# A shared root for two norms: ten GpSimd instructions become four steps on ScalarE and GpSimd, in a new written-out order

## The chip, the cores and the metric

The kernel runs on one core of a Trainium2 chip. The metric is the time of one execution in microseconds (us), taken on the device. Engines are named as in the profile: PE is TensorE's matmul, PEld its weight load, DVE is VectorE, ACT is ScalarE, POOL is GpSimd, SP is SyncE.

## What is computed

Two layers on an image batch x of shape 4 x 256 x 256 x 64 (batch, height, width, channels), float32. Cut to what matters:

```python
def ln(x, g, b):                      # norm over the 64 channels
    mu = mean(x, -1); var = mean((x - mu)**2, -1)
    return (x - mu) * rsqrt(var + 1e-3) * g + b

# layer 0
h  = ln(x, g1, b1) @ w_te + b_te                    # 64 -> 128 channels
F  = fft2(h)                                        # over height and width
fc = gelu(concat(F.real, F.imag) @ w_fc + b_fc)     # 256 -> 256
sp = ifft2(fc[..., :128] + 1j * fc[..., 128:]).real
x1 = x + sp @ w_tp + b_tp
h2 = ln(x1, g2, b2) @ w_fe + b_fe
d  = gelu(depthwise_conv3x3(h2) + b_dw)
x2 = x1 + d @ w_fp + b_fp
# layer 1: moving average over height, plus a filter of the rest with
# complex weights in the frequency domain; here one 256 x 256 matrix per channel
out = layer1(x2)
```

There are two norms: the first feeds the forward transform, the second feeds the 3 x 3 convolution. Each needs one over the square root of a variance for every pixel. The change is about how that root is computed.

## The kernel before

**Tiling and stages.** The work is cut into three kinds of pieces, and all three run in a pipeline. *Forward chunks* f(n), 32 per image, 128 in all: load four columns of x (`fl`), norm, half-sums, and the transform along the height (`y0`, `y1`), evicted by `yt0`, `yt1` and stored to memory. *Pairs* k, 65 per image, 260 in all: transform along the width (`x`), copy to SBUF (`xs`), the mixing matmuls (`m0`, `m1`), evictions (`gc0`, `gc1`), sums and differences on VectorE (`b0`, `b1`), Gelu on ScalarE (`g0`, `g1`), a sum on GpSimd (`p0`, `p1`), the projection `z` with its copy `zs`, a transpose `w` with its copy `zt`, and the way back along the width (`u`, `us`, `uc`, and `uf`, which stores u). *Convolution chunks* c(n), 32 per image: load u (`ul`, or `UL` for an image's first chunk) and x (`xl`, `XL`), back along the height (`s`), residual (`r0`, `r1`), second norm, transposes (`t0`, `t1`) with copies (`tt0`, `tt1`), row sums on GpSimd (`T0`, `T1`), products (`gm`, `gh`, `em`, `eh`), their evictions (`gc_0`, `gc_1`, `ec0`, `ec1`) and sums (`cf0`, `cf1`, `sp0`, `sp1`), Gelu (`a0`, `a1`), projection (`o0`, `o1`, copies `fs0`, `fs1`), transposes back (`ft0`, `ft1`) and the final sum and store (`st0`, `st1`). Layer 1 comes after all this, from about 3900 us.

**The order of the work** is written out by hand. A list of operations with offsets rules one period n; an entry such as `m0:2` means "do m0 up to index 2 beyond this period's base" (for pairs the base is 2(n - 35), for the way back n - 35, else n). There are lists for four stretches: SPECTRUM (forward chunks and pairs), FULL (all three kinds together: the stretch "beside the first transform", periods 71 to 131), MIXED (pairs and convolution, 132 to 169), CONV (convolution alone). `do(op, k)` runs an operation once for every index up to k, and first whatever FOLLOWS says must come ahead of it (`fx fp` means that fx needs fp of the same index). If no PSUM bank is free, the operation that frees the oldest one is pulled forward (`make_room`). PE, DVE, ACT and POOL run strictly in the order in which the program emits their instructions. Period 103 has no convolution chunk, since an image's first chunk needs the whole way back of its image.

**The norms.** `statistics` makes the operations of both norms. For the first norm (side 0) they are `fq fr fR fm fM fp` and then `fx`, for the second (side 1) `cq cr cR cm cM cp` and then `cx`: square (ACT, line 275), sum (DVE, line 279), the mean's square put beside the squares (ACT, lines 284 and 285), variance (DVE, line 290), start of the root (DVE, line 309), root (POOL), and the scaling of the data by the root (POOL, line 352). In the stretch FULL a forward chunk and a convolution chunk share a *round* (`get`): whichever sum comes first opens the round, the other side joins it. Then `cM` makes an integer seed for 32 columns (16 of each side), and `cp` refines it with ten GpSimd instructions, lines 330 to 340, two steps of a Newton kind. `fM` and `fp` of side 0 do nothing there. Elsewhere side 0 takes the power -0.5 in one GpSimd instruction (line 325), and side 1 the ten instructions with 16 columns. `rooted`, called by the scaling, takes the power for one chunk if its root isn't there yet, and clears the open round.

Of the kernel before, what the change touches and what calls it, by code (L numbers as in the profile page):

```python
# [11 lines left out]
F32 = mybir.dt.float32  # L12
I32 = mybir.dt.int32
AF = mybir.ActivationFunctionType
ALU = mybir.AluOpType
# [4 lines left out]
P = 128  # L20
# [116 lines left out]
def conv_seq_kernel(ctx: ExitStack, tc: tile.TileContext, a: dict, tables: bass.AP, out: bass.AP):  # L137
    nc = tc.nc
    x = a["x"]
# [4 lines left out]
    shared = ctx.enter_context(tc.tile_pool(name="shared", bufs=1))  # L144
# [57 lines left out]
    def const(shape, name):  # L202
        return consts.tile(shape, F32, tag=name, name=name)
# [19 lines left out]
    make_identity(nc, ident)  # L223
    minus_half = const([P, 1], "minus_half")
    nc.vector.memset(minus_half, -0.5)

    wp = const([P, 2 * HID], "wp")
    b_fc = const([P, 2], "b_fc")
# [13 lines left out]
    edge_rows = const([P, 2], "edge_rows")  # L242

    ROWS = 16
    joint = {"on": False, "open": None}
# [4 lines left out]
    def statistics(index, src, name, side):  # L250

        state = {}
        own = slice(side * ROWS, (side + 1) * ROWS)
        both = slice(0, 2 * ROWS)

        def get(j):
            if j not in state:
                round_ = joint["open"] if joint["on"] else None
                if round_ is None or side in round_["sides"]:
                    round_ = {"sides": set(), "done": set(), "has": set()}  # L260
                    for tag, bufs in (("total", 3), ("var", 3), ("seed", 3)):
                        round_[tag] = shared.tile(
                            [P, 2 * ROWS], F32, tag=tag, name=f"{tag}_{name(j)}", bufs=bufs
                        )
                    joint["open"] = round_ if joint["on"] else None
                else:
                    joint["open"] = None
                round_["sides"].add(side)
                round_[side] = j, index
                state[j] = round_  # L270
            return state[j]

        def square(j):
# [18 lines left out]
        def cols_of(j, alone):  # L292

            s = get(j)
            if alone:
                return s, own
            if side == 0:
                return s, None if joint["on"] or len(s["sides"]) == 2 else own
            if joint["open"] is s:
                joint["open"] = None  # L300
            if 0 not in s["has"]:
                s["has"].add("apart")
            return s, own if "apart" in s["has"] else both

        def start_root(j):
            s, cols = cols_of(j, False)
            if cols is not None and side:
                var, seed = s["var"][:, cols], s["seed"][:, cols]
                nc.vector.tensor_scalar(
                    seed.bitcast(I32), var.bitcast(I32), -0.5, float(0x5F3759DF), ALU.mult, ALU.add  # L310
                )

        def root(j, alone=False):
            s, cols = cols_of(j, alone)
            if cols is None:
                return
            n = cols.stop - cols.start
# [4 lines left out]
            var, seed, rstd = s["var"][:, cols], s["seed"][:, cols], rstd[:, cols]  # L322
            state.pop(j)
            if alone or not side:
                nc.gpsimd.tensor_tensor(rstd, var, minus_half.to_broadcast([P, n]), ALU.pow)
                return
            t = shared.tile([P, 2, 2 * ROWS], F32, tag="newton", name=f"newton_{name(j)}", bufs=1)
            t0, t1 = t[:, 0, cols], t[:, 1, cols]
            tt, ts = nc.gpsimd.tensor_tensor, nc.gpsimd.tensor_scalar
            tt(t0, seed, seed, ALU.mult)  # L330
# [6 lines left out]
            ts(t1, t0, 0.375, -1.25, ALU.mult, ALU.add)  # L337
            tt(t1, t1, t0, ALU.mult)
            ts(t1, t1, 1.875, None, ALU.add)
            tt(rstd, t1, rstd, ALU.mult)  # L340

        def rooted(j):
# [5 lines left out]
        return (square, add, less_mean, variance, start_root, root), rooted  # L348

    def scale(src, dst, rstd):  # L350
        n = src.shape[1]
# [140 lines left out]
    def forward_h(pool):  # L492
# [104 lines left out]
        def part(f, i):  # L597
# [2 lines left out]
        both = (("fh", halves_h), ("y", transform), ("yt", evict))  # L600
        return {
            "fl": load,
            **dict(zip(("fq", "fr", "fR", "fm", "fM", "fp"), stats)),
            "fx": scaled,
            "fa": halves,
            "fb": quarters,
# [289 lines left out]
    def convolution(pool, pairs):  # L896
# [386 lines left out]
        def when(f, is_first):  # L1283
# [10 lines left out]
            "s": back_h,  # L1294
            "r0": residual_even,
            "r1": residual_odd,
            **dict(zip(("cq", "cr", "cR", "cm", "cM", "cp"), stats)),
# [194 lines left out]
    def is_late(j):  # L1492
# [2 lines left out]


    FOLLOWS = """
        fq fl | fr fl | fR fr fq | fm fq fR | fM fm | fp fM | fx fp | fa fx y0:-1 y1:-1 | fb fa
# [3 lines left out]
        cc cl | c0 UL | xl st0:-6 st1:-6 | XL st0:-6 st1:-6 | s ul UL c0 | r0 s xl XL | r1 r0 | cq r1 | cr r1 | cR cr cq | cm cq cR | cM cm | cp cM  # L1502
# [18 lines left out]
    for line in FOLLOWS.replace("\n", "|").split("|"):  # L1521
# [3 lines left out]


    FULL = numbered("""
        gc1:1 b1:1 w:-2 cm:-1 gh:-4 gc_0:-4 cf0:-4 a1:-5 m0:1 cr:-1 gc0:1 zs:-1 b0:1 t0:-2 tt0:-2 fl
        fp:-1 fq fr fh0:-2 u:-1 us:-1 ul t1:-2 s cl uc:-1 fm cc:-1 tt1:-2 x:2 xl XL r0 zt:-2 w:-1
        g0:1 zt:-1 gc_1:-4 o1:-5 x:3 xs:2 fs1:-5 cR:-1 g1:1 r1 cq m0:2 o0:-5 p1 fR fx:-1 sp0:-4  # L1530
        sp1:-4 xs:3 fh1:-2 y0:-2 yt0:-2 fs0:-5 fM z ft0:-5 cM:-1 ft1:-5 cf1:-4 gc0:2 zs b0:2 m1:2
        gc1:2 st0:-5 y1:-2 yt1:-2 T0:-2 T1:-2 p1:1 Ta:-2 a0:-4 em:-3 g0:2 b1:2 eh:-3 fa:-1 fb:-1
        ec0:-3 ec1:-3 m1:3 p0:1 z:1 st1:-5 cp:-1 gm:-3 g1:2 uf:-1 p0:2 cx:-1 UL:1
    """)

    MIXED = numbered("""
        t0:-2 a0:-5 xs:1 zt:-3 gm:-4 t1:-2 tt0:-2 a1:-5 p0:-2 p1:-2 z:-2 zs:-2 gh:-4 uf:-2 cM:-1
        p0:-1 gc_0:-4 cf0:-4 g1:-1 cp:-1 m1 gc1 b1 s cl tt1:-2 r0 gc_1:-4 m0 gc0 m0:1 p1:-1 z:-1
        gc0:1 r1 x:2 b0 xs:2 o1:-5 fs1:-5 u:-1 o0:-5 T0:-2 x:3 cq b0:1 us:-1 fs0:-5 g0 cr cR uc:-1
        w:-2 ul:1 xl XL ft0:-5 zs:-1 st0:-5 ft1:-5 st1:-5 em:-3 g0:1 T1:-2 Ta:-2 eh:-3 zt:-2 ec0:-3  # L1540
        ec1:-3 m1:1 sp0:-4 sp1:-4 cx:-1 w:-1 cf1:-4 gc1:1 g1 b1:1 cm cc:-1 UL:1
    """)

    CONV = numbered("""
# [195 lines left out]
```

## Time and profile before

| | |
|---|---|
| time, median of 3 runs | 4371.74 us (4369.35 to 4373.44) |
| the profiled execution | 4370.57 us |
| its span, first to last instruction | 4368.8 us |
| PE, DVE, ACT, POOL busy over the span | 96%, 79%, 66%, 76% |
| granted TensorE clock, mean | 0.985 |
| MB read, written | 364.81, 286.00 |

A row of the profile names a line of the program, the engine, the operation, the tiles written and read, their shape and type and the count; after the bar come the busy time in us and the mean of one in ns, and after a second bar the idle time of the engine just ahead of them and what ended it. A busy PE isn't PE at its peak, since matmuls are pipelined and their ends are modelled. The chain of work goes back from the last instruction to whatever released it; each piece has its start, its length and what it was.

### The profile page before, as it was taken

How to read it: one execution, taken by the hardware profiler on the slowest of the kernel's cores; microseconds unless marked ns; L12 is line 12 of the kernel's file. 1: busy time of each engine (PE TensorE's matmuls, PEld its weight loads, DVE VectorE, ACT ScalarE, POOL GpSimd, SP SyncE). 2: the span in 40 equal slices, each digit the busy share in tenths (PEclk: the TensorE clock that was granted, in tenths of full speed). 3: DMA queues.
4: the chain of work that ended last, by engine and by line, in shares of the span. 5: the costliest groups of instructions: out<-in, count | busy, mean ns of one | idle time of the engine just before them, and what ended most of it. 6: DMA issues, size and time to landing. Idle time of an engine off the chain costs nothing.

```text
span 4368.8 us, 67589 instructions
## 1 busy us (share of the span) xinstructions
PE 4183.0 (96%) x22443; PEld 2308.1 (53%) x22443; DVE 3453.4 (79%) x5227; ACT 2892.5 (66%) x5121; POOL 3315.0 (76%) x3509
## 2 busy tenths in 40 slices
PE   8989999889999999899999999999998799999999
PEld 4544444345555555455555566666665466664444
DVE  6968999689999988898888877888887699972222
ACT  3338998677777777677777777888886366641111
POOL 6869999699999999799999877888887588850000
PEclk9999999999999999999999999999999899999999
DMA  6664555434444444444444343444433534439886
GB/s 187 210 188 140 160 160 161 139 102 132 134 136 135 131 124 129 125 127 135 135 136 126 111 112 97 117 111 111 117 102 82 174 105 113 117 91 372 343 344 230
DMA packets 763907, 655.30 MB, mean 150 GB/s; under 512 B 46413, under 2 KB 657695, under 8 KB 755240
## 3 DMA queue, kind: packets, MB, share of 16 engines
q1 hardware_dynamic: 726696, 583.84, 45.5%
q10 hardware_dynamic: 36864, 67.13, 4.0%
q8 instruction: 181, 2.97, 0.3%
q14 instruction: 166, 1.36, 0.1%
HBM read 364.81 MB, written 286.00 MB: 149 GB/s over the span
## 4 chain that ended last, share of the span: by engine, by line
PE 78%; DVE 9%; POOL 4%; ACT 4%; DMA 3%; issue 2%; SPq 1%; DVEq 0%; POOLq 0%; ACTq 0%
PE ps_p L692 10%; PE ps_o L1446 10%; PE ps_h_c L1108 9%; PE ps_h_c L1122 5%; PE ps_x L667 5%; PE ps_f_c L1225 5%; PE ps_u L798 5%; PE ps_s_c L983 5%; PE ps_y L557 4%; PE ps_z L747 4%; PE ps_hh_c L1108 4%; PE ps_zt L765 3%; PE ps_t_c L1030 3%; PE ps_ft_c L1250 2%; PE ps_hh_c L1122 2%
## 5 line engine op out<-in xcount | busy, mean ns | idle before, releaser
L712 DVE TENSOR_TENSOR g<-ps_p,g 128x512 f32<-128x512 f32 x1040 | 707.6, 683 | 131.1 <-ACT g L706 110.1
L723 POOL TENSOR_TENSOR g<-g 128x512 f32<-128x512 f32 (+1 forms) x520 | 677.0, 1313 | 126.3 <-ACT g L717 115.9
L717 ACT ACTIVATE g<-g,b_fc 128x1024 f32<-128x1024 f32 (+1 forms) x520 | 600.3, 1156 | 3.2 <-DVE g L712 3.1
L692 PE MATMUL ps_p<-xs,wp 64*128 64x512 f32 (+1 forms) x2080 | 566.5, 616 | 13.1 <-ACT xs L682 7.2
L1108 PE MATMUL ps_h_c<-td,wc_main 128*128 128x256 f32 x2048 | 506.8, 390 | 0.7 <-ACT zs L755 0.3
L1108 PEld LDWEIGHTS ps_h_c<-td,wc_main 128*128 128x128 f32 x2048 | 369.7, 192 | 143.2 <-ACT h_c L1142 41.4
L706 ACT COPY g<-ps_p 128x512 f32<-128x512 f32 (+1 forms) x520 | 304.4, 585 | 211.1 <-PE ps_p L692 140.8
L1446 PE MATMUL ps_o<-xc,mt 128*128 128x512 f32 x1024 | 441.5, 594 | 1.2 <-DVE oc L1460 1.2
L1218 ACT ACTIVATE h_c<-h_c,b_conv 128x1024 f32<-128x1024 f32 x256 | 295.5, 1156 | 128.3 <-DVE h_c L1187 51.0
L1460 DVE TENSOR_SCALAR oc<-ps_o,b_fp 128x512 f32<-128x512 f32 x128 | 93.4, 749 | 347.1 <-DMA out_dram<-oc 175.4
L1070 POOL TENSOR_TENSOR td<-tt 128x512 f32<-128x512 f32 x256 | 324.6, 1290 | 10.0
L551 POOL TENSOR_TENSOR xb<-xt 128x512 f32<-128x512 f32 x224 | 286.2, 1285 | 56.4 <-DVE xt L544 37.2
L1446 PEld LDWEIGHTS ps_o<-xc,mt 128*128 128x128 f32 x1024 | 195.1, 191 | 247.0 <-issue 236.6
L1458 ACT ACTIVATE oc<-ps_o,b_fp 128x512 f32<-128x512 f32 x128 | 86.1, 686 | 358.6 <-PE ps_o L1446 190.8
L667 PEld LDWEIGHTS ps_x<-tab,yb 128*64 128x64 f32 x4064 | 229.1, 137 | 153.3 <-issue 43.5
L1122 PE MATMUL ps_h_c<-td,wc_half 64*128 64x256 f32 (+1 forms) x2048 | 293.2, 401 | 2.4 <-POOL td L1074 1.0
L1264 DVE TENSOR_TENSOR st<-x_c,ps_ft_c 128x256 f32<-128x256 f32 x512 | 259.8, 596 | 40.4 <-PE ps_ft_c L1250 40.4
L1225 PE MATMUL ps_f_c<-h_c,w_fp 128*64 128x512 f32 x1024 | 273.7, 621 | 15.8 <-ACT h_c L1218 14.6
L747 PE MATMUL ps_z<-g,w_tp 128*64 128x512 f32 x1024 | 275.8, 610 | 13.3 <-POOL g L723 9.0
L983 PE MATMUL ps_s_c<-uc_c,tab 64*128 64x512 f32 x1024 | 260.8, 622 | 21.5 <-DVE uc_c L932 13.3
L692 PEld LDWEIGHTS ps_p<-xs,wp 64*128 64x128 f32 x2080 | 185.1, 186 | 182.1 <-issue 67.8
L557 PE MATMUL ps_y<-xb,tab 128*64 128x512 f32 x1024 | 265.3, 610 | 12.6 <-POOL xb L551 10.3
(189 smaller groups left out, 9654.3 us busy)
## 6 DMA issues: line engine op xcount, KB each, us to landing
y_d<-yt SPq DMA_DIRECT2D x256, 256.0 KB, 2.6
yb<-y_d SPq DMA_DIRECT2D x256, 256.0 KB, 4.2
u_d<-ut SPq DMA_DIRECT2D x256, 256.0 KB, 3.9
x_c<-in_x_dram SPq DMA_DIRECT2D x512, 128.0 KB, 3.2
x_d<-st SPq DMA_DIRECT2D x128, 512.0 KB, 4.8
xc<-x_d SPq DMA_DIRECT2D x64, 1024.0 KB, 8.1
out_dram<-oc ACTq DMA_DIRECT2D x256, 256.0 KB, 5.7
xt<-in_x_dram SPq DMA_DIRECT2D x504, 128.0 KB, 2.5
```

Of the source, the lines that this page charges most:

```text
L557: nc.tensor.matmul(ps[i * C : (i + 1) * C], dh[:, m, i * C : (i + 1) * C], sums[j][:, i], start=True, stop=True,)
L667: nc.tensor.matmul(ps[r * C : (r + 1) * C, j * N + t * P : j * N + (t + 1) * P], blk[:, t, k, r * C : (r + 1) * C], tb[:, t, :], start=Tru ...
L692: nc.tensor.matmul(ps[:, :nf], wp[rows, cols], rhs[rows], start=True, stop=r == 1 or not pr["special"],)
L712: nc.vector.tensor_tensor(gt[:, i], re, gt[:, 1], op)
L717: nc.scalar.activation(g, g, AF.Gelu, bias=b_fc[:, half : half + 1])
L723: nc.gpsimd.tensor_tensor(g[:, 0], g[:, 0], g[:, 1], op)
L747: nc.tensor.matmul(ps[r * C : (r + 1) * C, :nf], w_tp, d[:, :nf], start=True, stop=True)
L983: nc.tensor.matmul(pss[i], tb[i * C : (i + 1) * C], uc[i * C : (i + 1) * C, ::-1, 1 - r, :] if down else uc[i * C : (i + 1) * C, :, r, :], ...
L1108: nc.tensor.matmul(product(j, k, par), wc_main[:, par, k, :], td[:, k, slots(j)].rearrange("p j q -> p (j q)"), start=k in (0, 1, 3), stop ...
L1122: nc.tensor.matmul(product(j, k, par)[:, dst.start * Q : dst.stop * Q], wc_half[lo : lo + C, k, :], td[lo : lo + C, k, src].rearrange("p j ...
L1225: nc.tensor.matmul(ps[par * C : (par + 1) * C], w_fp, gs[j][:, :, par, i0 : i0 + 2, :].rearrange("p r j q -> p r (j q)"), start=True, stop ...
L1446: nc.tensor.matmul(ps[:, :nf], mts[i // CM][:, i % CM, t, to * P : (to + 1) * P], xc[:, t, :, :, i, :], start=t == 0, stop=t == 1,)
```

## The change

In the stretch FULL the shared root is no longer ten GpSimd instructions in one operation, but four operations of the list, `cA`, `cB`, `cC` and `cp` (with `fA`, `fB`, `fC`, `fp` of side 0, which do nothing there). Each has one or two activations on ScalarE and one multiplication on GpSimd, on 32 columns. The second step's polynomial is brought into the form of a square plus a constant. The list FULL is new throughout. MIXED is the same cyclic order, begun at another place, with the offsets that this brings; the last index of `gm` and `em` in it sets from which chunk on the convolution takes its late form (166, before 167). Outside FULL the roots are computed as before. The scratch tile `newton` has two buffers instead of one.

```diff
+    affine = const([P, 3], "affine")
+    nc.vector.memset(affine[:, 0:1], 1.5)
+    nc.vector.memset(affine[:, 1:2], -(0.375**0.5) * 5.0 / 3.0)
+    nc.vector.memset(affine[:, 2:3], 5.0 / 6.0)
...
         def start_root(j):
-            s, cols = cols_of(j, False)
-            if cols is not None and side:
+            s = get(j)
+            s["whole", side] = joint["whole"] or side == 0 and not joint["on"]
+            s["spread", side] = joint["on"]
+            cols = s["cols", side] = None if s["whole", side] else cols_of(s)
+            if cols is not None:
...
+        def square_seed(j):
...
+            a, t = (s["t", side][:, i, cols] for i in range(2))
+            nc.scalar.activation(a, s["seed"][:, cols], AF.Square)
+            nc.gpsimd.tensor_tensor(t, a, s["var"][:, cols], ALU.mult)
+
+        def first_step(j):
...
+            s["rstd", side] = roots(s, j)
+            a, t = (s["t", side][:, i, cols] for i in range(2))
+            nc.scalar.activation(a, t, AF.Identity, bias=affine[:, 0:1], scale=-0.5)
+            nc.gpsimd.tensor_tensor(
+                s["rstd", side][:, cols], a, s["seed"][:, cols], ALU.mult
+            )
+
+        def square_step(j):
...
+            a, t = (s["t", side][:, i, cols] for i in range(2))
+            nc.scalar.activation(a, s["rstd", side][:, cols], AF.Square)
+            nc.gpsimd.tensor_tensor(t, a, s["var"][:, cols], ALU.mult)
+
+        def root(j, alone=False):
+            s = get(j)
+            if alone or s["whole", side]:
...
+            if not s["spread", side]:
+                in_place(roots(s, j)[:, cols], s["var"][:, cols], s["seed"][:, cols], j)
+                return
+            a, t = (s["t", side][:, i, cols] for i in range(2))
+            rstd = s["rstd", side][:, cols]
+            nc.scalar.activation(a, t, AF.Square, bias=affine[:, 1:2], scale=0.375**0.5)
+            nc.scalar.activation(a, a, AF.Identity, bias=affine[:, 2:3])
+            nc.gpsimd.tensor_tensor(rstd, a, rstd, ALU.mult)
...
     FULL = numbered("""
-        gc1:1 b1:1 w:-2 cm:-1 gh:-4 gc_0:-4 cf0:-4 a1:-5 m0:1 cr:-1 gc0:1 zs:-1 b0:1 t0:-2 tt0:-2 fl
-        fp:-1 fq fr fh0:-2 u:-1 us:-1 ul t1:-2 s cl uc:-1 fm cc:-1 tt1:-2 x:2 xl XL r0 zt:-2 w:-1
-        g0:1 zt:-1 gc_1:-4 o1:-5 x:3 xs:2 fs1:-5 cR:-1 g1:1 r1 cq m0:2 o0:-5 p1 fR fx:-1 sp0:-4
-        sp1:-4 xs:3 fh1:-2 y0:-2 yt0:-2 fs0:-5 fM z ft0:-5 cM:-1 ft1:-5 cf1:-4 gc0:2 zs b0:2 m1:2
-        gc1:2 st0:-5 y1:-2 yt1:-2 T0:-2 T1:-2 p1:1 Ta:-2 a0:-4 em:-3 g0:2 b1:2 eh:-3 fa:-1 fb:-1
-        ec0:-3 ec1:-3 m1:3 p0:1 z:1 st1:-5 cp:-1 gm:-3 g1:2 uf:-1 p0:2 cx:-1 UL:1
+        b0:2 ec1:-4 cm:-1 gh:-4 m0:3 gc_0:-4 ec0:-4 a0:-5 cf0:-4 p0:1 g0:2 m1:3 fr:1 fh1:-1 p1:1 z:1
+        gc1:3 gc0:3 b1:3 fq:1 o0:-5 fs0:-5 o1:-5 cx:-2 fs1:-5 fh0:-1 b0:3 y0:-1 ft0:-5 g1:2 sp0:-4 w
+        st0:-5 zs:1 p0:2 fR:1 fm:1 cc:-1 yt0:-1 ft1:-5 fC:-1 p1:2 fp xl XL t1:-2 ul fM:1 fA st1:-5
+        sp1:-4 tt1:-2 s cl t0:-2 w:1 gc_1:-4 tt0:-2 r0 r1 cM:-1 fx T0:-2 T1:-2 z:2 m1:4 gc1:4 fB
+        y1:-1 yt1:-1 uf:-1 zs:2 cr UL:1 x:5 xs:5 g0:3 u x:6 b1:4 us m0:4 zt xs:6 gc0:4 zt:1 cf1:-4
+        fl:2 a1:-4 cA:-1 Ta:-2 cB:-1 cq gm:-3 fa fb cC:-1 cR cp:-1 g1:3 uc em:-3 eh:-3
     """)
...
-        joint["on"] = names is FULL
+        joint["on"], joint["whole"] = names is FULL, names is SPECTRUM
```

In FOLLOWS, `fp fM` and `cp cM` become the chains `fA fM | fB fA | fC fB | fp fC` and `cA cM | cB cA | cC cB | cp cC`.

More of the change, by code (lines that the diff above doesn't have):

```diff
@@ L244, in conv_seq_kernel @@
     ROWS = 16
-    joint = {"on": False, "open": None}
+    joint = {"on": False, "open": None, "whole": True}
     sq = shared.tile([P, ROWS, C + 2], F32, tag="sq", name="sq")
@@ L290, in variance, with cols_of @@
             nc.vector.tensor_reduce(get(j)["var"][:, own], sq, AX.X, ALU.add)
[L292 to L296, printed above, removed]
+        def cols_of(s):
             if side == 0:
-                return s, None if joint["on"] or len(s["sides"]) == 2 else own
+                if joint["on"] or len(s["sides"]) == 2:
+                    return None
+                if joint["open"] is s:
+                    joint["open"] = None
+                return own
             if joint["open"] is s:
                 joint["open"] = None
-            if 0 not in s["has"]:
-                s["has"].add("apart")
-            return s, own if "apart" in s["has"] else both
+            return both if 0 in s["has"] else own
         def start_root(j):
-            s, cols = cols_of(j, False)
-            if cols is not None and side:
+            s = get(j)
[3 more added lines that the diff above has]
+            if cols is not None:
                 var, seed = s["var"][:, cols], s["seed"][:, cols]
@@ L311, in start_root, with roots @@
                 )
[L313 to L317, printed above, removed]
+        def roots(s, j):
+            n = s["cols", side].stop - s["cols", side].start
             rstd = shared.tile([P, 2 * ROWS], F32, tag="rstd", name=f"rstd_{name(j)}", bufs=3)
@@ L321, in root, with in_place @@
                 index_[k] = rstd[:, at * ROWS : (at + 1) * ROWS]
[L322 to L328, printed above, removed]
+            return rstd
+        def in_place(rstd, var, seed, j):
+            t = shared.tile([P, 2, 2 * ROWS], F32, tag="newton", name=f"newton_{name(j)}", bufs=2)
+            t0, t1 = (t[:, i, : var.shape[1]] for i in range(2))
             tt, ts = nc.gpsimd.tensor_tensor, nc.gpsimd.tensor_scalar
@@ L340, in root @@
             tt(rstd, t1, rstd, ALU.mult)
+        def square_seed(j):
+            s = get(j)
+            cols = s["cols", side]
+            if cols is None or not s["spread", side]:
+                return
+            s["t", side] = shared.tile(
+                [P, 2, 2 * ROWS], F32, tag="newton", name=f"newton_{name(j)}", bufs=2
+            )
+            a, t = (s["t", side][:, i, cols] for i in range(2))
+            nc.scalar.activation(a, s["seed"][:, cols], AF.Square)
+            nc.gpsimd.tensor_tensor(t, a, s["var"][:, cols], ALU.mult)
@@ new lines, in first_step @@
+        def first_step(j):
+            s = get(j)
+            cols = s["cols", side]
+            if cols is None or not s["spread", side]:
+                return
+            s["rstd", side] = roots(s, j)
[3 more added lines that the diff above has]
+                s["rstd", side][:, cols], a, s["seed"][:, cols], ALU.mult
+            )
+        def square_step(j):
+            s = get(j)
+            cols = s["cols", side]
+            if cols is None or not s["spread", side]:
+                return
+            a, t = (s["t", side][:, i, cols] for i in range(2))
+            nc.scalar.activation(a, s["rstd", side][:, cols], AF.Square)
+            nc.gpsimd.tensor_tensor(t, a, s["var"][:, cols], ALU.mult)
@@ new lines, in root @@
+        def root(j, alone=False):
+            s = get(j)
+            if alone or s["whole", side]:
+                rstd = shared.tile([P, 2 * ROWS], F32, tag="rstd", name=f"rstd_{name(j)}", bufs=3)
+                index[j] = rstd[:, own]
+                nc.gpsimd.tensor_tensor(
+                    rstd[:, own], s["var"][:, own], minus_half.to_broadcast([P, ROWS]), ALU.pow
+                )
+                return
+            cols = s["cols", side]
+            if cols is None:
+                return
+            if not s["spread", side]:
+                in_place(roots(s, j)[:, cols], s["var"][:, cols], s["seed"][:, cols], j)
+                return
+            a, t = (s["t", side][:, i, cols] for i in range(2))
[3 more added lines that the diff above has]
+            nc.gpsimd.tensor_tensor(rstd, a, rstd, ALU.mult)
@@ L346, in rooted @@
             return index.pop(j)
-        return (square, add, less_mean, variance, start_root, root), rooted
+        steps = square_seed, first_step, square_step, root
+        return (square, add, less_mean, variance, start_root, *steps), rooted
     def scale(src, dst, rstd):
@@ L602, in forward_h @@
             "fl": load,
-            **dict(zip(("fq", "fr", "fR", "fm", "fM", "fp"), stats)),
+            **dict(zip(("fq", "fr", "fR", "fm", "fM", "fA", "fB", "fC", "fp"), stats)),
             "fx": scaled,
@@ L1296, in convolution @@
             "r1": residual_odd,
-            **dict(zip(("cq", "cr", "cR", "cm", "cM", "cp"), stats)),
+            **dict(zip(("cq", "cr", "cR", "cm", "cM", "cA", "cB", "cC", "cp"), stats)),
             "cx": scaled,
@@ L1497, in conv_seq_kernel @@
     FOLLOWS = """
-        fq fl | fr fl | fR fr fq | fm fq fR | fM fm | fp fM | fx fp | fa fx y0:-1 y1:-1 | fb fa
+        fq fl | fr fl | fR fr fq | fm fq fR | fM fm | fA fM | fB fA | fC fB | fp fC | fx fp | fa fx y0:-1 y1:-1 | fb fa
         fh0 fb | fh1 fb | y0 fh0 fh1 | y1 fh0 fh1 | yt0 y0 yt1:-1 | yt1 y1 yt0:-1
@@ L1501, in conv_seq_kernel @@
         p0 g0 | p1 g1 | z p0 p1 | zs z w:-1 | w zs | zt w | us u uc:-1 | uc us uf:-1 | uf uc
-        cc cl | c0 UL | xl st0:-6 st1:-6 | XL st0:-6 st1:-6 | s ul UL c0 | r0 s xl XL | r1 r0 | cq r1 | cr r1 | cR cr cq | cm cq cR | cM cm | cp cM
+        cc cl | c0 UL | xl st0:-6 st1:-6 | XL st0:-6 st1:-6 | s ul UL c0 | r0 s xl XL | r1 r0 | cq r1 | cr r1 | cR cr cq | cm cq cR | cM cm | cA cM | cB cA | cC cB | cp cC
         cx cp t0:-1 t1:-1 | t0 cx | t1 cx | tt0 t0 T0:-1 T1:-1 | tt1 t1 T0:-1 T1:-1
@@ L1527, in conv_seq_kernel @@
     FULL = numbered("""
-        gc1:1 b1:1 w:-2 cm:-1 gh:-4 gc_0:-4 cf0:-4 a1:-5 m0:1 cr:-1 gc0:1 zs:-1 b0:1 t0:-2 tt0:-2 fl
-        fp:-1 fq fr fh0:-2 u:-1 us:-1 ul t1:-2 s cl uc:-1 fm cc:-1 tt1:-2 x:2 xl XL r0 zt:-2 w:-1
-        g0:1 zt:-1 gc_1:-4 o1:-5 x:3 xs:2 fs1:-5 cR:-1 g1:1 r1 cq m0:2 o0:-5 p1 fR fx:-1 sp0:-4
-        sp1:-4 xs:3 fh1:-2 y0:-2 yt0:-2 fs0:-5 fM z ft0:-5 cM:-1 ft1:-5 cf1:-4 gc0:2 zs b0:2 m1:2
-        gc1:2 st0:-5 y1:-2 yt1:-2 T0:-2 T1:-2 p1:1 Ta:-2 a0:-4 em:-3 g0:2 b1:2 eh:-3 fa:-1 fb:-1
-        ec0:-3 ec1:-3 m1:3 p0:1 z:1 st1:-5 cp:-1 gm:-3 g1:2 uf:-1 p0:2 cx:-1 UL:1
+        b0:2 ec1:-4 cm:-1 gh:-4 m0:3 gc_0:-4 ec0:-4 a0:-5 cf0:-4 p0:1 g0:2 m1:3 fr:1 fh1:-1 p1:1 z:1
[4 more added lines that the diff above has]
+        fl:2 a1:-4 cA:-1 Ta:-2 cB:-1 cq gm:-3 fa fb cC:-1 cR cp:-1 g1:3 uc em:-3 eh:-3
     """)
     MIXED = numbered("""
[L1537 to L1541, printed above, removed]
+        XL:-1 ft0:-6 zs:-3 st0:-6 ft1:-6 st1:-6 em:-4 g0:-1 T1:-3 Ta:-3 eh:-4 zt:-4 ec0:-4 ec1:-4
+        m1:-1 sp0:-5 sp1:-5 cx:-2 w:-3 cf1:-5 gc1:-1 g1:-2 b1:-1 cm:-1 cc:-2 UL t0:-2 a0:-5 xs:1
+        zt:-3 gm:-4 t1:-2 tt0:-2 a1:-5 p0:-2 p1:-2 z:-2 zs:-2 gh:-4 uf:-2 cM:-1 p0:-1 gc_0:-4 cf0:-4
+        g1:-1 cp:-1 m1 gc1 b1 s cl tt1:-2 r0 gc_1:-4 m0 gc0 m0:1 p1:-1 z:-1 gc0:1 r1 x:2 b0 xs:2
+        o1:-5 fs1:-5 u:-1 o0:-5 T0:-2 x:3 cq b0:1 us:-1 fs0:-5 g0 cr cR uc:-1 w:-2 ul:1 xl
     """)
```

## The prediction, made before the result was known

> **What bounds the kernel now.** I read the page first, then busy time by stage, then the rows of GpSimd and ScalarE in the steady part of the changed stretch, then the chain of work there. The page says that TensorE and GpSimd are both busy nearly everywhere before 3900 us:
>
> ```profile
> PE 4183.0 (96%) x22443; PEld 2308.1 (53%) x22443; DVE 3453.4 (79%) x5227; ACT 2892.5 (66%) x5121; POOL 3315.0 (76%) x3509
> ```
>
> By stage, each row 12 or 14 periods long (first the list FULL, then MIXED; columns: length, then busy time of PE, PEld, DVE, ACT and POOL):
>
> ```profile
> 1111.80:1443.80 332.00, 327.90 (x1922) 177.58 (x1922) 305.01 (x446) 258.27 (x465) 317.20 (x338) 1.00 0.48 134
> 2847.90:3178.20 330.30, 330.30 (x2132) 211.56 (x2130) 278.09 (x436) 275.47 (x474) 273.20 (x351) 1.00 0.41 112
> ```
>
> The starts of the second norm's square (line 275) in the timeline are 27.67 us apart in FULL and 23.6 in MIXED. So a FULL period of 27.67 us holds PE 27.3, GpSimd 26.4, VectorE 25.4, ScalarE 21.5. GpSimd's remaining 1.2 us are pauses of about 0.08 us between dependent instructions: GpSimd is full, and TensorE all but full beside it. The root is ten rows of GpSimd (columns after the bar: busy us, mean ns, idle before):
>
> ```profile
> L337 POOL TENSOR_SCALAR newton_c<-newton_c 128x32 f32<-128x32 f32 x13 | 15.1, 1158 | 1.1
> L330 POOL TENSOR_TENSOR newton_c<-seed_c 128x32 f32<-128x32 f32 x13 | 8.6, 660 | 0.0
> ...
> L338 POOL TENSOR_TENSOR newton_c<-newton_c 128x32 f32<-128x32 f32 x13 | 4.3, 334 | 1.1
> ...
> L340 POOL TENSOR_TENSOR rstd_c<-newton_c,rstd_c 128x32 f32<-128x32 f32 x13 | 3.3, 253 | 1.1
> ```
>
> All ten: 64.6 us busy and 9.6 us of pauses in 13 periods, 4.97 + 0.74 = 5.7 us each. Uncontended, one takes 0.25 us (last row). For TensorE, four pieces of one period's chain matter:
>
> ```profile
> 1032.86 1.06 PE ps_p L692 x4
> ...
> 1037.91 0.86 PE ps_p L692 x4
> ...
> 1039.78 1.93 PE ps_h_c L1108 x8
> 1041.71 1.73 PE ps_hh_c L1108 x8
> ```
>
> The same work costs 0.20 us more when the piece before it used the array in another split (64 rows by 128, 128 by 64, or whole).
>
> **What the Trainium skill says.** "SBUF — State Buffer", section "SBUF: two separate sides": the port pair of VectorE and GpSimd is an exclusive lock, taken by a VectorE instruction with two SBUF inputs; the other blocks for the whole instruction. The trace agrees: at 1009 to 1014 us the root's instructions take 0.57 to 1.23 us while VectorE adds the halves and quarters of lines 524 and 544, and 0.25 us otherwise. "TensorEngine Tiling (Array Packing)", section "Key Properties": changing the tiling mode drains TensorE; the pieces above agree at 0.15 to 0.20 us. "ScalarE: Activation LUTs", section "Table sets: the hidden batching unit": identity is in every set. The trace has two table loads in all, at 6.6 and 329.4 us; Square runs after the second, and so does the biased Identity of line 1458. So the new activations load nothing.
>
> **The change, part by part.** *Root.* GpSimd loses ten instructions, 5.7 us, and gets four multiplications. ScalarE gets five activations of 32 columns. Price: line 285, a scaled 16-column one, takes 0.232 us here. The page "ScalarE: Activation LUTs", section "What ACT_TABLE_LOAD costs", gives 0.83 ns an element and 93 ns for a bias pointer: estimate 0.24 for the two Squares without bias, 0.33 for the three with one, 1.5 us in all. ScalarE goes from 21.5 to 23.0 of 27.7 us: room.
>
> Working the new list through by its own rules, GpSimd has nothing else between the four multiplications, so the chain counts at its length: multiply 0.25, hop 0.06 and Identity 0.31; ScalarE then does the norm's large square (1.10) and the next Square (0.24); beside GpSimd's third product it does two small ones (0.5), then two of 0.31; last product 0.3. Sum 3.4 us, estimated. If three products each wait for one VectorE add of 0.68 us (fa and fb stand there in the list), 5.4. I take 4.0. GpSimd: 27.65 - 5.7 + 4.0 = 26.0 us (25.4 to 27.4).
>
> *What the waits hold up.* ScalarE now waits inside the chain for GpSimd. Behind it stand the square of 1.1 us, g1's Gelu, and then the evictions ec and gc_ of the next period; TensorE's next matmuls need those banks. Before the second step ScalarE has some 12 instructions (6.5 us, copies start 0.48 us apart) beside GpSimd's six row sums (7.9 us with pauses), so it arrives about 1 us early and waits that long in each period; its 4.7 us of room cover that. Without that room it would be 1 us of the period.
>
> *Order of FULL.* Before, TensorE's order of a period is zt, gh, m0, t0, u, t1, s, x, zt, o1, x, m0, o0, y0, z, ft, m1, y1, em, eh, m1, z, gm: 17 changes of split. In the new list: gh, m0, m1 | z, o0, o1, y0 | ft0, zt, ft1, t1 | s | t0, zt | z | m1 | y1, x, u, x | m0 | gm, em | eh: 10. The pieces of that period's chain sum to 26.5 us, with one z of 0.86 that runs beside its end to 27.4; what they exceed their shortest form by is 3.2 in all, 0.19 a change. Without changes 24.15; with 10 changes 26.05. VectorE needs about 24.9 without lock waits (25.4 less some 0.5 on lines 309 and 524). So the period cannot fall under 26.0, and three engines meet near there. MIXED has no y (1.72) and 6 changes, by the same sum 23.55, and takes 23.6: TensorE can run almost bare. In FULL three engines are near the bound, and I allow 1.5% for it: 26.05 x 1.015 = 26.4 us, so 1.3 us saved (bounds 1.7 and 0.2).
>
> *How many periods.* FULL rules periods 71 to 131, 61 of them; less three of filling, two around the missing chunk (103), four without forward chunk: 52. 52 x 1.3 = 68 us.
>
> *Pairing.* Now f(n) is loaded two chunks ahead, so fx comes before the shared root of its old partner. Followed through: the first fx finds no root, takes the power of line 325 (2.9 us) and clears the open round, after which c(n) pairs with f(n+2) and all later ones are shared. Some four extra powers, at entry and after the hole: 12 us of GpSimd, hidden where TensorE is waiting anyway (its clock there is 0.81 to 0.91); 0, at most +12.
>
> *Ends of the stretch.* Pairs run up to six ahead (before: three), so period 71 does some three pairs more, each some 6 us, and periods 132 and 133 have nearly none; that moves 15 to 20 us and saves none. After the hole, the first chunk's load (UL) is now issued 0.7 of a period before its use, not 0.15: the wait there (two periods take 61.6 us) may lose up to 8. Taken together 0, bounds -15 to +15.
>
> *Queues.* SyncE's loads of x for the forward norm move from the list's start to its end, behind the spill of u that waits for VectorE; they then have a period to land (median 2.5 us). ul stands some 12 us before s once SyncE runs ahead. Cost 0; without that cover, about 3 us of landing a period. MIXED is the same cycle turned; one more chunk takes the late form: 0. Three memsets of constants at the start lie beside the first loads: 0, bare 0.5 us.
>
> *Sum.* The profiled execution took 4370.6 us (span 4368.8 and 1.8 around it), 1.2 under the median of the three runs. 4370.6 - 68 + 1.2 = 4304.
>
> **Rivals.** *A, as above*: period 26.2 to 26.9, 4277 to 4330 (0.50). *B, the chain stays as long as the ten instructions*: lock waits at each product, ScalarE late. For it: the ten are inflated from 2.5 to 5.0 us by just these adds. Against: four products meet fewer adds. The period stays at 27.3 to 27.7: 4354 to 4372 (0.19). *C, more*: 26.0 and a shorter wait at the hole and entry: 4371 - 52 x 1.65 - 15 = 4270 (0.19). For it: MIXED runs on TensorE almost bare. *D, slower*: the chain couples two queues. Should ScalarE come 2 us late to the first Square because of its own waits for TensorE and VectorE, and the locks take 0.6 beyond the 4.0, GpSimd idles through both: 26.0 + 2.6 = 28.6, 52 x 0.95 = 49 us more, 4421. It decides from 1.65 us of added wait on. For it: nothing stands between the products on GpSimd. Against: ScalarE's room (0.09). *E, the pairing never locks*: 2.9 us of power in each period on top of 26.0 gives 28.9, 4436 (0.03); against it, the round-clearing above.
>
> **Numbers.** About 0.2% is what a measurement can tell from no change: 4363 to 4380. A, C and half of B lie below, A + C + 0.10 = 0.79; same 0.09; slower D + E = 0.12. Range 4262 to 4366: it takes in A and most of C and B; outside are D, E and the tails of B and C, about 0.2.
>
> **What would show it.** Right: squares of line 275 some 26.4 us apart, GpSimd's newton rows down from 5.7 to about 2 us a period with idle time that ScalarE ended, matmul pieces with fewer 0.2 us starts, no further table load, no power row inside the stretch. Wrong: a period still near 27.6 with GpSimd waiting for ScalarE at the products (B), TensorE waiting for evictions behind the chain (D), 50 more powers (E), or gains eaten before 900 or near 1750 us.

## The result, and the profile after

| | before | after |
|---|---|---|
| median | 4371.42 us (4366.35 to 4378.38, 20 runs) | 4364.96 us (4357.78 to 4368.28, 20 runs) |
| the profiled execution, its span | 4370.57, 4368.8 us | 4357.78, 4356.0 us |

The ratio is 0.9984 [0.9977, 0.9991]: 6.5 us less, or 0.16%. That is a small gain, but the interval leaves out 1. The forecast was 68 us less. The profiled execution of the changed kernel is the fastest of its 20, 7 us under their median; positions in time below come from it.

Busy time over the whole span, from the page of the changed kernel:

```profile
PE 4171.1 (96%) x22443; PEld 2320.0 (53%) x22443; DVE 3452.7 (79%) x5234; ACT 2961.9 (68%) x5414; POOL 3159.4 (73%) x3151
```

GpSimd lost 156 us of work and 358 instructions, ScalarE gained 69 us. The mechanism is in place, the time isn't. By stage, the same two as before, twelve periods of FULL and fourteen of MIXED (length, then PE, PEld, DVE, ACT, POOL):

```profile
1091.50:1414.50 323.00, 320.62 (x1923) 178.27 (x1922) 300.54 (x445) 273.19 (x526) 283.56 (x265) 1.00 0.50 138
```

```profile
2848.00:3180.00 332.00, 332.00 (x2139) 213.25 (x2138) 279.98 (x437) 276.52 (x475) 274.33 (x352) 1.00 0.41 112
```

A FULL period is 26.92 us long (27.67 before; forecast 26.4), with 26.7 us of TensorE in it. MIXED shows TensorE without a gap, as before. The four products of the root on GpSimd, and the one row that grew, a row sum (line 1125 here, 1067 before, when its mean was 1275 ns):

```profile
L1125 POOL TENSOR_TENSOR tt<-tt 128x512 f32<-128x512 f32 x12 | 26.7, 2229 | 0.9
L355 POOL TENSOR_TENSOR newton_c<-newton_c,var_c 128x32 f32<-128x32 f32 x12 | 5.5, 460 | 9.6 <-ACT newton_c L354 9.6
L365 POOL TENSOR_TENSOR rstd_c<-newton_c,seed_c 128x32 f32<-128x32 f32 x13 | 3.8, 293 | 5.6 <-ACT newton_c L364 5.6
L376 POOL TENSOR_TENSOR newton_c<-newton_c,var_c 128x32 f32<-128x32 f32 x12 | 3.0, 252 | 9.3 <-ACT newton_c L375 9.3
L397 POOL TENSOR_TENSOR rstd_c<-newton_c,rstd_c 128x32 f32<-128x32 f32 x12 | 3.0, 252 | 10.5 <-ACT newton_c L396 10.5
```

The products are 1.26 us a period and their waits for ScalarE (third column) 2.9: the chain is 4.2 us long. The chain of work at the end of one FULL period, in order of time:

```profile
1140.75 1.11 PE ps_p L750 x4
1141.86 0.02 issue
1141.88 0.59 ACT xs L740
1142.47 0.04 issue
1142.52 1.56 PE ps_h_c L1166 x6
```

TensorE has done m0 (`ps_p`) and comes to gm (`ps_h_c`), which needs banks that the copies `zt` and `xs` on ScalarE set free. Two of gm's first eight matmuls start once `zt` is copied; the other six wait for `xs` of line 740, which in turn may overwrite its buffer only when m0, just ahead, has read it. The chain shows 0.65 us between m0 and the third of these eight. Since two matmuls ran in it, TensorE loses less. The two lines of the changed kernel, and the same two of e12 below, where nothing waits, give it by their starts:

```profile
1141.74 2.34 PE L1166 MATMUL ps_h_c<-td,wc_main 128*128 128x256 f32 x8
1143.92 1.89 PE L1166 MATMUL ps_hh_c<-td,wc_main 128*128 128x256 f32 x8
```

```profile
1213.42 1.99 PE L1167 MATMUL ps_h_c<-td,wc_main 128*128 128x256 f32 x8
1215.25 1.89 PE L1167 MATMUL ps_hh_c<-td,wc_main 128*128 128x256 f32 x8
```

That is 2.18 against 1.83 us, a loss of 0.35.

**Where the time went.** The starts of the second norm's square, chunk by chunk, against those of before:

| convolution chunk (of 128) | period | after minus before, us |
|---|---|---|
| 0 | 71 | +32.0 |
| 4 | 75 | +38.4 |
| 16 | 87 | +28.9 |
| 31, 34 | 102, 106 | +17.3, +18.8 |
| 55 | 127 | +5.2 |
| 60 | 132 | -8.5 |
| 127 | the last | -13.4 |

So three sums: the entry of the stretch loses 38, the steady part gives back 33 (0.65 a period on average over chunks 4 to 55, with the hole; 0.75 over chunks 9 to 21), its end 14. The entry in windows of 20 us, first the kernel before, then the changed one (PE, PEld, DVE, ACT, POOL, then the granted clock):

```profile
840.00:860.00 20.00, 15.27 (x78) 5.72 (x76) 10.20 (x14) 9.87 (x14) 10.15 (x8) 0.87 0.25 79
860.00:880.00 20.00, 16.18 (x84) 6.09 (x80) 17.17 (x28) 13.64 (x23) 14.69 (x18) 0.91 0.39 116
880.00:900.00 20.00, 16.88 (x84) 6.39 (x84) 16.31 (x20) 14.06 (x28) 18.32 (x14) 0.83 0.27 79
```

```profile
840.00:860.00 20.00, 13.94 (x27) 3.35 (x24) 9.96 (x13) 6.72 (x12) 8.21 (x7) 0.50 0.10 26
860.00:880.00 20.00, 16.84 (x94) 7.40 (x94) 13.71 (x17) 11.00 (x22) 7.39 (x5) 0.85 0.35 106
880.00:900.00 20.00, 17.94 (x86) 7.57 (x86) 16.66 (x31) 11.40 (x21) 9.98 (x7) 0.91 0.40 116
```

Look at the counts in brackets: in the first 20 us TensorE does 27 matmuls instead of 78. They are not all of one size, but it looks nearly as busy also because its clock fell to 0.50: a y matmul takes 1.08 us there and 0.62 in the steady part. The kernel before has a weak stretch too, 20 us earlier (32 matmuls from 820 to 840, where the changed kernel has 56); over the whole from 820 to 900 it is 278 matmuls against 263. A piece of the entry's chain of work shows how the engines take turns there:

```profile
833.91 2.08 ACT g L775 x2
836.00 0.48 ACT g L764
836.50 0.70 DVE g L770
837.23 0.70 DVE g L770
```

In the three windows above GpSimd does 25.6 us of work in 60 us (8.21 + 7.39 + 9.98), against 43.2.

### The profile page after: what moved, and what is told of

It is laid out like the page before. It is cut to its first block, busy times and chain, and to the rows that moved or that the text cites. A ratio compares the mean times of both kernels' runs of the same rounds, so it can differ in the third digit from the quotient of the medians.

```text
span 4356.0 us, 67401 instructions
## 1 busy us (share of the span) xinstructions
PE 4171.1 (96%) x22443; PEld 2320.0 (53%) x22443; DVE 3452.7 (79%) x5234; ACT 2961.9 (68%) x5414; POOL 3159.4 (73%) x3151
## 4 chain that ended last, share of the span: by engine, by line
PE 66%; POOL 12%; DVE 7%; ACT 5%; DMA 5%; issue 4%; SPq 2%; POOLq 0%; ACTq 0%; DVEq 0%
PE ps_o L1504 9%; PE ps_p L750 8%; PE ps_h_c L1166 6%; PE ps_s_c L1041 5%; PE ps_y L615 5%; PE ps_z L805 4%; PE ps_x L725 4%; PE ps_u L856 4%; PE ps_h_c L1180 4%; POOL xb L609 3%; PE ps_f_c L1283 3%; PE ps_hh_c L1166 3%; PE ps_zt L823 3%; PE ps_t_c L1088 3%; POOL g L781 3%
## 5 line engine op out<-in xcount | busy, mean ns | idle before, releaser
L1166 PE MATMUL ps_h_c<-td,wc_main 128*128 128x256 f32 x2048 | 516.5, 391 | 6.7 <-DVE g L770 1.4
L805 PE MATMUL ps_z<-g,w_tp 128*64 128x512 f32 x1024 | 290.9, 619 | 28.3 <-POOL g L781 21.3
L615 PE MATMUL ps_y<-xb,tab 128*64 128x512 f32 x1024 | 274.8, 629 | 28.2 <-POOL xb L609 22.8
L1180 PE MATMUL ps_h_c<-td,wc_half 64*128 64x256 f32 (+1 forms) x2048 | 279.1, 395 | 3.7 <-POOL td L1132 2.4
```

The costliest lines, as they stand in the source:

```text
L615: nc.tensor.matmul(ps[i * C : (i + 1) * C], dh[:, m, i * C : (i + 1) * C], sums[j][:, i], start=True, stop=True,)
L805: nc.tensor.matmul(ps[r * C : (r + 1) * C, :nf], w_tp, d[:, :nf], start=True, stop=True)
L1166: nc.tensor.matmul(product(j, k, par), wc_main[:, par, k, :], td[:, k, slots(j)].rearrange("p j q -> p (j q)"), start=k in (0, 1, 3), stop ...
L1180: nc.tensor.matmul(product(j, k, par)[:, dst.start * Q : dst.stop * Q], wc_half[lo : lo + C, k, :], td[lo : lo + C, k, src].rearrange("p j ...
```

## The experiments

Two questions: what holds the steady period at 26.9 us, and what costs the entry. My theory was that GpSimd holds the period (chain 4.2, row sum 0.95 longer) and that TensorE's wait ahead of gm, by chance, ends at the same length. The rival has one bound alone. For the entry: pairs pulled one after another, or work merely done earlier. All ratios are against the kernel before. Periods are means of twelve, from the same two chunks (9 and 21) in each run, from one profiled execution each; five kernels with the same list FULL (the changed one, e4, e7, e13, e14) give 26.88 to 26.92, so 0.04 is no difference.

**e1, the new order with the old root.**

```diff
-            s["spread", side] = joint["on"]
+            s["spread", side] = False
```

> The new list with the old root: ten GpSimd instructions in cp. Theory (GpSimd still sets the period, now by the chain of four products and the waits between them): without products and chain waits GpSimd has 22.4 us of a period plus 0.4 of pauses; the ten instructions add 0.7 of pauses and 2.5 to 5.0 us, depending on the lock: period 26.0 to 28.5, some 27.2, and no wait for ScalarE; total about 4371 (4350 to 4410). Rival (the order of TensorE sets 26.9): the period stays at 26.9, 4365.

Measured: 4385.74 us, ratio 1.0035 [1.0022, 1.0047], period 27.40. The new order by itself gains 0.27 us a period and loses more than that at the entry (33 us at chunk 4). The new root gives the other 0.48 us of the period, and in all 4385.7 - 4365.0 = 20.8 us.

**e2, the new root in the old order.** The lists FULL and MIXED are those of before; FOLLOWS then places the four steps directly behind each other where `cp` stood.

> The old lists FULL and MIXED with the new root: the four steps follow one another at the place of the old cp. Theory: GpSimd falls to about 24.5 us a period, and the old TensorE order with 17 changes of split binds at 27.2 to 27.4: total about 4352, entry and exit as before. Rival (the changes of split are no need, GpSimd alone set 27.67): period 25.5 to 26, total about 4280.

Measured: 4534.22 us, ratio 1.0374 [1.0359, 1.0388], mean period 30.7. Both numbers missed. What GpSimd and the others wait for in eleven periods (total, times, longest):

```profile
POOL newton_c L355 <- ACT newton_c L354: 56.0, 11, 5.3
DVE g L770 <- ACT g L764: 39.7, 22, 3.0
PEld ps_t_c L1088 <- POOL g L781: 33.3, 11, 3.0
```

GpSimd stands 5.1 us a period at the first product, since ScalarE reaches its Square late, and TensorE waits behind it. This is rival D, in the order that was not made for the new root.

**e3, the second norm's large square behind the chain.**

```diff
-        fl:2 a1:-4 cA:-1 Ta:-2 cB:-1 cq gm:-3 fa fb cC:-1 cR cp:-1 g1:3 uc em:-3 eh:-3
+        fl:2 a1:-4 cA:-1 Ta:-2 cB:-1 gm:-3 fa fb cC:-1 cp:-1 cq cR g1:3 uc em:-3 eh:-3
```

> The new kernel with the second norm's large square and its mean (cq, cR) behind the chain instead of inside it. Theory (the chain's length on GpSimd sets the period): ScalarE's 1.05 us go out of the chain, GpSimd's waits in it fall from 2.9 to about 2.0 us, the period from 26.9 to 26.0 to 26.2; total about 4327. Rival (TensorE's order sets 26.9): nothing moves, 4365.

Measured: 4359.82 us, ratio 0.9975 [0.9965, 0.9984], period 26.88. The third product (line 376) no longer waits for the 1.04 us square: its waits in twelve periods fell from 9.3 to 4.1 us, while those of the first product rose from 9.6 to 13.9. The period fell by 0.04, so the chain alone isn't the bound.

**e9, the two y products behind m0.** TensorE then has work while ScalarE frees the banks.

```diff
-        y1:-1 yt1:-1 uf:-1 zs:2 cr UL:1 x:5 xs:5 g0:3 u x:6 b1:4 us m0:4 zt xs:6 gc0:4 zt:1 cf1:-4
+        uf:-1 zs:2 cr UL:1 x:5 xs:5 g0:3 u x:6 b1:4 us m0:4 y1:-1 zt xs:6 gc0:4 yt1:-1 zt:1 cf1:-4
```

> Only the two y products stand behind m0; the chain of the root is as in the changed kernel. Two-bounds theory: GpSimd's 26.9 us remain, so the period stays at 26.8 to 26.9 and the time at 4360 to 4366, and only together with the moved square does it fall. If TensorE's wait alone was the bound: period 26.4, time 4340.

Measured: 4363.26 us, ratio 0.9978 [0.9972, 0.9985], period 26.91. TensorE's wait alone isn't the bound either.

**e6, both edits (e3 and e9).**

> The second norm's large square stands behind the chain of the root, and the two y products stand behind m0, so that TensorE has work while ScalarE frees the banks that gm writes. Two-bounds theory (GpSimd's chain and TensorE's wait of 0.6 us for zt and xs coincide at 26.9 us): taking both away gives a period of 26.3 to 26.45 and 4335 to 4345. One-bound theory (GpSimd alone holds 26.9, its waits only change place): the period stays at 26.85 and the time at 4360.

Measured: 4351.93 us, ratio 0.9956 [0.9943, 0.997], period 26.65. Neither edit moved the period by more than 0.04 us, both together by 0.27. Two bounds lie side by side. The gain is smaller than I expected.

**e11, the refinement of the shared roots left out.** The four steps are gone in FULL (the first three functions return at once, the fourth changes as follows), and one small copy of the seed stands for the root.

```diff
-            nc.scalar.activation(a, t, AF.Square, bias=affine[:, 1:2], scale=0.375**0.5)
-            nc.scalar.activation(a, a, AF.Identity, bias=affine[:, 2:3])
-            nc.gpsimd.tensor_tensor(rstd, a, rstd, ALU.mult)
+            nc.gpsimd.tensor_scalar(
+                roots(s, j)[:, cols], s["seed"][:, cols], 1.0, None, ALU.mult
+            )
```

> Left out: the refinement of the shared roots; in FULL the first estimate is taken as the root, by one small copy on GpSimd, so the normalized values are off by some per cent. The order is that of the changed kernel. GpSimd then needs some 23.4 us a period, so what remains of the period is TensorE's and the waits around it. Two-bounds theory: TensorE's 26.15 us plus its 0.6 us at the banks of gm hold the period at 26.7 to 26.8, and the time is 4356 to 4362. One-bound theory (GpSimd alone holds 26.9): the period falls to 26.2 to 26.3 and the time to some 4330.

Measured: 4355.67 us, ratio 0.9958 [0.9944, 0.9971], period 26.88. With no refinement at all the period is only 0.04 us shorter than with it. This chain of work from e11 (its lines stand one further down) is why:

```profile
1210.70 1.11 PE ps_p L751 x4
1211.81 0.02 issue
1211.83 0.59 ACT xs L741
1212.43 0.04 issue
1212.47 1.56 PE ps_h_c L1167 x6
```

The rest of that period's chain is TensorE, but for 0.13 us ahead of `zt`. GpSimd, no longer waiting in the root's chain, now waits 2.9 us a period for ScalarE's Gelu and VectorE's sums. The wait for `xs` is not caused by the root. Summed from the starts of its matmuls, this period is 24.15 us of shortest forms and 1.9 of the ten changes of split (the prediction's two terms), 0.35 lost at gm, 0.3 ahead of the second `zt`, whose cause I don't know, and 0.1 in small delays.

**e12, e11 with y behind m0 as well.**

> Left out as in the run before: the refinement of the shared roots. The two y products stand behind m0 as well, so that gm's banks are free in time. Two-bounds theory: nothing but TensorE's own 26.15 us is left, period 26.15 to 26.3, time 4325 to 4335 with the entry as in the changed kernel. If the period stays at 26.6, another wait than the banks of gm holds TensorE.

Measured: 4341.25 us, ratio 0.9927 [0.9912, 0.9943], period 26.65, not 26.15 to 26.3. The chain of one period has no wait left but 0.12 us (ahead of `zt`):

```profile
1208.83 1.72 PE ps_u L857 x8
1210.55 0.87 PE ps_x L726 x16
1211.42 1.06 PE ps_p L751 x4
1212.48 1.01 PE ps_y L616 x4
1213.49 1.92 PE ps_h_c L1167 x8
```

Moving y broke a run of equal splits. y takes 1.01 behind m0 as it did behind m1, but x, which now stands behind a product of another split, takes 1.02 instead of 0.87. So the 0.35 us lost at gm were exchanged for 0.15 of one more change: 26.88 - 0.35 + 0.15 = 26.68, near the measured 26.65. It also explains e6, which has the same period: 26.65 is TensorE's bound there.

**e16 and e15, VectorE's sum of the back halves moved.** `uf` (line 920) adds two SBUF tiles while GpSimd does the row sum of line 1125. It goes to the root's chain, where GpSimd waits anyway; alone in e16, with y behind m0 in e15.

```diff
-        y1:-1 yt1:-1 uf:-1 zs:2 cr UL:1
+        y1:-1 yt1:-1 zs:2 cr UL:1
...
-        fl:2 a1:-4 cA:-1 Ta:-2 cB:-1
+        fl:2 a1:-4 cA:-1 uf:-1 Ta:-2 cB:-1
```

> Only VectorE's sum of the back halves is moved to beside the chain of the root. Two-bounds theory: GpSimd is eased, but TensorE with its wait at the banks of gm still holds 26.85 to 26.9 us, so the time stays at 4358 to 4365. If GpSimd alone holds the period: 26.2 to 26.5 and 4335 to 4345.

> The y products stand behind m0, and VectorE's sum of the back halves (the operation uf) is moved from beside GpSimd's row sums to beside the chain of the root, where GpSimd waits for ScalarE some 2.9 us a period. If the lock is what makes the row sum take 2.23 us, that row goes back to 1.28, GpSimd's bound falls from 26.9 to about 26.0 to 26.4, and TensorE's bare 26.65 decides: period 26.65, some 4350. If the row sum is slow for another reason, it stays at 2.23 us, the period at 26.9 and the time at 4363.

Measured: e16 4364.52 us, ratio 0.9984 [0.9977, 0.999], period 27.10; e15 4346.93 us, ratio 0.9943 [0.9929, 0.9956], period 26.73. The row of e15:

```profile
L1125 POOL TENSOR_TENSOR tt<-tt 128x512 f32<-128x512 f32 x12 | 15.4, 1281 | 0.9
```

The row sum is back from 2229 to 1281 ns, so it was the lock. In e9 the period stayed at 26.91 with the lock on the row sum, here it comes near to TensorE's 26.65. It is not shown that GpSimd alone was the bound: `uf` also leaves its place in VectorE's order, and in e9 the chain of work runs through VectorE from 1164.5 to 1172.1 us. But e6 leaves `uf` where it is, eases only the root's chain, and gains too. So the second bound is a loop of GpSimd, ScalarE and VectorE, with the root's chain in it and, most likely, the row sum. TensorE feels it where y waits for GpSimd's half-sums: from the first matmul of o to the first of y it takes 1.79 us on average in e3, e6, e11 and e12, and 2.00 in the changed kernel. With `uf` alone nothing is gained (the first product then waits 1.7 us for ScalarE, and TensorE still waits for `xs`). Its period is 0.2 longer, which I had not expected; the same stretch up to y takes 2.27 us there, and why GpSimd comes later stays open.

**e4, the entry stretched.** The pairs' lead grows over four periods instead of at once (START is period 71).

```diff
-                base = 2 * (n - S0)
+                base = 2 * (n - S0) - (max(0, START + 3 - n) if names is FULL else 0)
```

> The new kernel with the pairs' lead brought in over four periods (3, 2, 1, 0 pairs less at periods 71 to 74), the rest unchanged. Theory (of the 32 us that the first convolution chunk is late, about half is a bubble: pairs pulled one after another while GpSimd is nearly idle and the clock falls to half): the entry wins 10 to 18 us, total about 4352. Rival (the 32 us are pairs moved from the end, given back there): 4365.

Measured: 4374.91 us, ratio 1.0008 [1.0001, 1.0014]. Both forecasts missed. At chunk 4 the loss is 47.8 us, 9 more than in the changed kernel. My reading, not tested further: a pulled chain in each of four periods costs more than one.

**e7, the lead in the order of the list before.** Ahead of period 71, the operations of two rounds of pairs and of one forward chunk run in SPECTRUM's order, which interleaves them; FULL then finds its three extra pairs done. `period` calls `lead` once, when n is 71.

```diff
+    def lead(n):
+        for k in (n, n + 1):
+            for op, at in SPECTRUM:
+                if op in PAIRS:
+                    do(op, 2 * (k - S0) + at)
+                elif op in forward and k == n:
+                    do(op, k + at)
```

> Before period 71 the new list runs in its place two rounds of the second chunks' operations in the order of the list of the stretch before, and one round of the forward chunk's; FULL then starts with its pairs already three ahead. Disorder theory (the 30 us lost at the entry come from the new list's long chain of three pairs being pulled one after another): the entry loses 10 us or less against the kernel before, and the time is some 4340. Moved-work theory (what is done early there is simply missing later, at the end of the stretch): entry still 30 late, exit still 14 early, time 4360 to 4370.

Measured: 4339.21 us, ratio 0.9928 [0.9916, 0.9941], period 26.91. At chunk 0 the loss is 7.7 us instead of 32.0, at chunk 4 18.8 instead of 38.4, and the end of the stretch still gives its 14 back. So the work moved is the same, and the order of it made up 20 us of the loss at chunk 4 of the profiled executions, 26 by the medians. The same window in e7 (its own weakest, 880 to 900 us, has 52 matmuls at 0.74):

```profile
840.00:860.00 20.00, 17.73 (x94) 6.88 (x90) 13.91 (x17) 9.86 (x17) 6.47 (x5) 0.84 0.31 87
```

94 matmuls at a clock of 0.84, where the changed kernel had 27 at 0.50.

**e13 and e14, the lead of the pairs alone, and of the forward chunk alone** (the other branch of `lead` is left out).

> Of the two rounds run ahead of period 71 only the second chunks' operations, not the forward chunk's. If the long chain of three pairs is what lost the time at the entry: as with both, some 4340. If it was the forward chunk, loaded and used at once: 4360 to 4365.

> Of the rounds run ahead of period 71 only the forward chunk's operations. If the chain of three pairs lost the time at the entry: no gain, 4360 to 4365. If the forward chunk did: 4340 to 4345.

Measured: e13 4343.04 us, ratio 0.9932 [0.9919, 0.9944]; e14 4371.93, ratio 0.9999 [0.9991, 1.0007]. It is the pairs: their lead alone gives 22 of the 26 us, that of the forward chunk alone loses 7.

**e10, all three: e3, e9 and e7.**

> Square behind the chain, y behind m0, and the entry run in the order of the list before. If the entry's 20 to 30 us and the period's 0.5 us are both real and separate, their gains add: some 4315 to 4325. If the entry is only moved work: 4335 to 4345. If neither is right: 4360.

Measured: 4321.69 us, ratio 0.9888 [0.9875, 0.9902], period 26.63. The two gains add (26 for the entry and 13 for the period make 4326). This version beats both kernels.

A third buffer for `xs`, which would take TensorE's wait away without a change of split, wasn't tried.

## Why the prediction was wrong

**What held.** ScalarE's five steps: forecast 1.5 us, measured 1.42 (238, 322, 212, 321 and 322 ns). The chain: forecast 4.0, measured 4.2. From the first product on it takes 3.4, as the sum in the prediction has it; the rest is a wait of 0.8 for the first Square, to which ScalarE, by the prediction's count, would come 1 us early. No table load was added. The power was taken 75 times in either kernel: none of the four extra ones. TensorE's shortest forms and its ten changes: forecast 26.05, and by the starts in e11 the same. D's mechanism exists (e2: GpSimd waits 5.1 us a period at the first product), and this list keeps it to 0.8. The missing chunk's two periods went from 61.6 to 60.5 us, but the next took 31.1 instead of 27.9, so that from chunk 31 to 34 some 4 us were lost against steady periods; the forecast had up to 8.

**First step that failed: "three engines meet near there ... I allow 1.5% for it: 26.05 x 1.015 = 26.4".** It was 26.92, so 0.65 to 0.75 us saved a period instead of 1.3, and 33 us instead of 68 over the stretch. The 1.5%, 0.4 us, stood for all waits. Two terms were missing, and easing either alone left 26.9.
- *TensorE*: 0.8 us of waits beside the 26.05, of them 0.35 at gm. I followed the order of the matmuls and their splits and not the banks: whose eviction frees the ones that gm takes, and what that eviction waits for. e11 shows that these waits alone hold 26.88.
- *GpSimd*: "27.65 - 5.7 + 4.0 = 26.0". The 5.7 held 2.5 us of lock waits, which I took away with the instructions. VectorE's adds are still there. The prediction named those of lines 524 and 544, but the longest root instruction in its stretch, 1.23 us, ran beside line 862 of the kernel before, which is `uf`:

```profile
1012.54 1.20 DVE L862 TENSOR_TENSOR ut<-ut,ut 128x1024 f32<-128x1024 f32 x1
1012.59 1.23 POOL L337 TENSOR_SCALAR newton_c<-newton_c 128x32 f32<-128x32 f32 x1
```

  The same add now meets a row sum and costs it 0.95 us. The Trainium skill, "SBUF — State Buffer", section "SBUF: two separate sides", says that the lock blocks the other engine for the whole instruction, whichever that is; e15 shows it here (2229 to 1281 ns). With 4.2 and 0.95 in it the sum reads 27.1; 26.92 was measured.

Each hides the other: e3, e9 and e16 ease one side and gain nothing that counts (26.88, 26.91, 27.10), e6 and e15 ease both and do (26.65, 26.73).

**Second step that failed: "Ends of the stretch ... Taken together 0, bounds -15 to +15".** It was +38 at the entry and -14 at the end, +24 in sum. The count of the work was right ("three pairs more ... moves 15 to 20 us, and saves none"), and the end did give 14 back. What I left out is how this work is emitted: period 71 pulls the chains of three pairs by FOLLOWS, each operation directly behind the one that it needs, so that all engines wait for each other in turn. In order it costs 20 to 26 us less (e7, e13).

The sum then reads, for the profiled execution: +38 - 33 - 14, and some 5 in what follows (in the other runs with this MIXED between 4 gained and 2 lost, so it may be chance), make -13 (4368.8 to 4356.0 us). Against the medians it is 6.5.

**The rivals.** B had the time (4354 to 4372) but not the reason: the chain did get shorter, and without any refinement the period would be the same. The gain is given back at two bounds and at the entry. C and E did not occur, and D only in e2. That 4365 lies inside the stated range (to 4366) is luck: it is B's time, without B's cause.

## What to carry to other kernels

Before a step is credited with its busy time, ask what its waits were: a lock wait that fell on the removed instructions can fall on their neighbours (here 0.95 of 2.5 us on one row). A new order has to be followed by its buffers as well as by its engines: for each matmul, who frees its bank and what that one waits for. Where a pipeline changes its lead at the seam of two lists, write out the filling; what a "run whatever it needs first" rule pulls in is a serial chain.

## What the runs showed of the hardware

- The granted TensorE clock fell to 0.50 for 20 us at the entry, when a serial chain left TensorE 27 matmuls in that time; busy time hid it (13.9 us against 15.3 with 78 matmuls at 0.87), since a y matmul took 1.08 us instead of 0.62. Counts of the same matmul show such a stretch, busy shares don't.
- The Trainium skill, "TensorEngine Tiling (Array Packing)", section "Key Properties", says that a change of the tiling mode drains TensorE. The runs put a price on it: the ten changes of a period in e11 come to 1.9 us by the starts of the matmuls, and the one more in e12 to 0.15 (x 1.02 instead of 0.87), which took back 0.15 of the 0.35 that the removed wait was worth.
